# A three-block transformer on one core: instructions moved between VectorE, ScalarE and TensorE, and a new order in the second and third block

## The chip, the cores and the metric

The kernel runs on one core of a Trainium2 chip. The metric is the time of one execution on the device in microseconds (us). Three runs of the kernel before gave 1351.33, 1355.53 and 1358.17 us; the median is 1355.53. The profile shows one further execution, and all durations come from it.

Engines are called as in the profile: PE is TensorE's matrix multiply and PEld its weight load, DVE is VectorE, ACT is ScalarE, POOL is GpSimd, and SP issues the DMAs. L846 is line 846 of the kernel before. Below L742 the changed kernel has other line numbers (the old L841 is L838 there).

## The reference: what is computed

Input is `x` with 32 sequences of 128 tokens and 144 channels, and one condition vector of 144 for each sequence. Four layers follow each other, all in fp32:

- L0, an attention block with 16 heads of 9 channels. Layer norm with shift and scale from the condition; queries and keys are normalised by head; softmax; projection; then an MLP of 576 with GELU. Both results are added to `x` with a gate.
- L1, a rotation. An orthonormal basis U of 64 columns comes from a QR decomposition of a weight, and for each sequence a matrix exponential R = expm(A) of a skew 64x64 matrix that depends on the condition; then `x + (x U R - x U) U^T`.
- L2, the attention block again, without normalised queries and keys.
- L3, the attention block again, whose MLP is a mixture of 4 experts: `gate_logits = xf @ w_gate`, the best two of the four logits, a softmax over them, and the weighted sum of two experts' MLPs.

```
gate_logits = xf @ w_gate                      # [tokens, 144] x [144, 4]
topk_logits, topk_idx = top_k(gate_logits, 2)
gates = softmax(topk_logits)
```

## The kernel before, in words

**Turns and gaps.** The order of all instructions is written out by hand. A loop runs over turns (`tick` in the code, from -6 to 112). In a turn one sequence `s0` has its scores computed, the sequence of the turn before, `s1`, has them computed a second time with the maximum subtracted and exponentiated, and the one before that, `s2`, is weighed with its values, divided by the sums and projected. The first block's sequences start in turns 0 to 31, the second block's in 35 to 66, the third block's in 67 to 98. L1, the rotation, lies between the first and the second block: its QR and its exponential are prepared in pieces during the first block.

Everything else is put into named gaps of the turns, and `fill(tick, gap)` emits what was put there. The gaps of a turn follow each other as

`a, e, t, [scores half 0], stats, [weigh], b0, b, den, pre1, [scores half 1], c, y1, y2, [maxima], z, [projection]`

with "d" ahead of the maxima in the first block and after "z" from turn 35 on (the "joined" turns). `put` places a function in a gap; within a gap functions run in the order in which they were put, that is by block and by group of four sequences. `put2` splits a function at its `yield` over two gaps. Each engine executes its instructions in this program order, so a place in the list is a place in every engine's queue. [...] All PSUM results but one come from a pool of seven banks, taken in rotation.

**The pieces that the change touches.**

- `scores` (L811 to L856): TensorE computes `ps_s` (plain scores) and `ps_w` (the shifted ones, from `q2` and `kT`), L841. VectorE takes the negative maximum by head of `ps_s` into `nm` (L846), ScalarE the exponential of `ps_w` into `pr` (L853).
- `largest_T` and `largest`: TensorE transposes `nm` (L800), VectorE adds it to the queries, `q2` (L805). The next turn's `ps_w` needs `q2`.
- First block, division by the softmax sums: `sums` (L877, gap after "den") transposes the weighed values on TensorE (L881), takes the reciprocal of the sums on VectorE (L884) and spreads it over the 16 slots of a head, 128x256, on VectorE (L886, tile `rdx`). `divide_T` (after "c") transposes `rdx` on TensorE (L906), `divide` (after "y1") multiplies on VectorE into `oT` (L911), and `project_out` at the turn's end needs `oT` (L932). In the joined turns `sums_by_blocks` does it on VectorE alone.
- First block, normalised queries and keys: `qk0_T` and `qk0_project` stand in gap "c". On ScalarE they are three scalings out of `ps_qkT` (L774 to L776) and a copy and a square out of `ps_qk` (L729, L730). `qk0_guess` (gap "e") makes the first guess of a reciprocal square root from the bits of the variance with two VectorE instructions (L742, L745).
- The exponential (`prep_expm`): powers of A, then two polynomial series with 8 coefficients in 128x1024 tiles (L531, L534), then four squarings for all sequences. Further squarings stand in a conditional block that runs where a row sum of A exceeds `THETA * 16`.
- Second and third block: `qk_chunks` (turn t0 - 2, gap "c") computes queries and keys of a group of four into four banks and ScalarE copies them, `qT` (L711) and one masked half of the keys `kT` (L713). `qk_masked` writes the other masked half from the same banks on VectorE (L719, gap "z").
- Third block: `gate_logits` (L1008 to L1015, turn t0 + 7, gap "den"), `expert_ranks` one turn later, `moe1` and `moe2`, the experts' two products. `shared_by_gate` transposes the gate weights (`ps_cw`) and VectorE multiplies them into the part of `hid` that two experts share (L1077); `moe2` of an even expert reads that part in its last product (L1089) and adds to `acc` with two VectorE instructions (L1093, L1095).

Of the kernel before, what the change touches and what calls it, by code (L numbers as in the profile page):

```python
# [8 lines left out]
F32 = mybir.dt.float32  # L9
# [21 lines left out]
E = 4  # L31
G = 4
# [1 line left out]
EPS = 1e-6  # L34
SCALE = HD**-0.5

THETA = 2.0
NSQ = 18
NSQ1 = 4
KP = 80  # L40
# [26 lines left out]
def tile_kernel(ctx: ExitStack, tc: tile.TileContext, a: dict, out: bass.AP):  # L67
# [11 lines left out]
    def bank(shape, name):  # L79

        n = 1
        for s in shape[1:]:
            n *= s
        t = ps_m.tile([128, 512], F32, tag="m", name=name)
        v = t[: shape[0], :n]
        if len(shape) == 3:
            v = v.rearrange("p (a b) -> p a b", b=shape[2])
        elif len(shape) == 4:
            v = v.rearrange("p (a b c) -> p a b c", b=shape[2], c=shape[3])
        return v  # L90
# [303 lines left out]
    def prep_expm():  # L394
# [132 lines left out]
        def series(co, name):  # L527

            lo, hi = mat(f"{name}_lo"), mat(f"{name}_hi", "hi")
            for t, cs_ in ((hi, co[4:]), (lo, co[:4])):  # L530
                nc.vector.tensor_scalar(t, pw1, cs_[1], None, ALU.mult)  # L531
                yield
                for c, x in ((cs_[0], i2b), (cs_[2], pw2), (cs_[3], pw3)):
                    nc.vector.scalar_tensor_tensor(t, x, c, t, ALU.mult, ALU.add)  # L534
                    yield
            yield from products(
                pw4, hi, f"ps_{name}",
                lambda bs, ps: nc.vector.tensor_tensor(lo[:, bs, :], lo[:, bs, :], ps, ALU.add),
            )
            return lo  # L540

        even = yield from series([(-1.0) ** k / fact[2 * k] for k in range(8)], "even")
        odd = yield from series([(-1.0) ** k / fact[2 * k + 1] for k in range(8)], "odd")
        rot, rotT = mat("rot", "pow3"), mat("rotT", "pow4")

        def sum_and_difference(bs, ps):
# [192 lines left out]
    def qk0_guess(s):  # L739
        va = st[s]["va"]  # L740
        y = small.tile([128, 32], F32, tag="qky", name=f"qky_{s}", bufs=2)
        nc.vector.tensor_scalar(  # L742
            y.bitcast(I32), va.bitcast(I32), 1, None, ALU.logical_shift_right
        )
        nc.vector.tensor_scalar(y.bitcast(I32), y.bitcast(I32), -1, RSQRT, ALU.mult, ALU.add)  # L745
        st[s]["y"] = y

    def qk0_newton(s, eng=nc.gpsimd):
# [128 lines left out]
    def sums(s):  # L877

        po = st[s]["ot"][:, : 2 * T].rearrange("p (t q) -> p t q", t=2)
        for t in range(2):  # L880
            nc.tensor.transpose(po[:, t, :], st[s]["on"][:, t, :], ident)  # L881
        den = po.rearrange("p t (s c) -> p t s c", c=SLOT)[:, :, :, ONE]
        rd = small.tile([128, 2, 8], F32, tag="rd", name=f"rd_{s}")
        nc.vector.reciprocal(rd, den)  # L884
        rdx = work.tile([128, 2, 8, SLOT], F32, tag="rdx", name=f"rdx_{s}")
        nc.vector.tensor_copy(rdx, rd.unsqueeze(3).to_broadcast([128, 2, 8, SLOT]))  # L886
        st[s]["rdx"] = rdx

    def sums_by_blocks(s):

# [10 lines left out]

    def divide_T(s):
        po = st[s]["ot"][:, : 2 * T].rearrange("p (t q) -> p t q", t=2)
        rdx = st[s].pop("rdx")
        for t in range(2):
            nc.tensor.transpose(po[:, t, :], rdx[:, t, :, :].rearrange("p s c -> p (s c)"), ident)  # L906

# [100 lines left out]
    def gate_logits(g):  # L1008
        gr[g]["lg"] = lg = small.tile([128, G, E], F32, tag="lg", name=f"lg_{g[1]}", bufs=2)
        hM, hR = gr[g]["hM_m"], gr[g]["hR_m"]  # L1010
        ps = bank([128, G, E], f"ps_g_{g[1]}")
        for i in range(G):
            nc.tensor.matmul(ps[:, i, :], hM[:, i, :], L3.wgate, start=True, stop=False)
            nc.tensor.matmul(ps[:, i, :], hR[:, i, :], L3.wgateR, start=False, stop=True)
        nc.vector.tensor_copy(lg, ps)  # L1015

    def expert_ranks(g):

# [183 lines left out]
    def put2(tick, gap, to, f, *args):  # L1202

        halves = []

        def first_half():
            halves.append(f(*args))
            next(halves[0])

        def second_half():  # L1210
            for _ in halves[0]:
                pass

        put(tick, gap, first_half)
        put(tick, to, second_half)

    for layer in range(3):
        ahead = 5 if layer == 0 else 6
        for n in range(NG):
            g = (layer, n)  # L1220
            t0 = first[layer] + n * G
            for i in range(G):
                s = layer * B + n * G + i
                at_a = t0 + i - ahead
                if layer == 1 and n == 0:
                    at_a = t0 - 4 + i // 2
                if layer == 1 and i == 0:
                    put(at_a - 2, "d", rotate_T, n)
                    put(at_a - 1, "b", rotate_in, n)
                    put(at_a - 1, "d", rotate, n)  # L1230
                stats[at_a].append((s, "a"))
                stats[t0 + i + 3].insert(0, (s, "m"))
                if layer < 2:
                    put(*((at_a, "d") if at_a != t0 + i - ahead else (at_a + 1, "b")), ln_T, s, "a")
                else:
                    put(at_a, "d", ln_T, s, "a")
                if layer == 0:
                    put(t0 + i + 4, "a", ln_T, s, "m")
                else:
                    put(t0 + i + 3, "d", ln_T, s, "m")  # L1240
                if layer == 0:
                    put(t0 + i - 3, "c", qk0_project, s)
                    put(t0 + i - 3, "z", qk0_variance, s)
                    put(t0 + i - 2, "e", qk0_guess, s)
                    if s == 0:
                        for gap in "bbc":
                            put(-2, gap, qk0_newton, s, nc.vector)
                    else:
                        for gap in ("b", "c", "y2"):
                            put(t0 + i - 2, gap, qk0_newton, s)  # L1250
                    put(t0 + i - 1, "b", qk0_divide, s)
                    put(t0 + i - 1, "c", qk0_T, s)
            if layer == 0:
                for i in (0, 2):
                    put(t0 + i // 2, "b", lambda g=g, i=i: list(values(g, i, 2)))
            elif layer == 1:
                put2(t0, "stats", "b", values, g, 0, 2, True)
                put2(t0 + 1, "stats", "b", values, g, 2, 2, True)
            else:
                put2(t0, "c", "c", values, g, 0, 2, True)  # L1260
                put2(t0 + 1, "den", "pre1", values, g, 2, 2)
            if layer:
                put2(t0 - 2, "c", "c", qk_chunks, g)
                put(t0 - 2, "z", qk_masked, g)
            if layer == 0:
                put2(t0 + 10, "stats", "b", mlp1, g, 0, (0, 1, 2), True)
                put2(t0 + 11, "d", "d", mlp1, g, 3, (3, SHARED), False)
                for i in range(G):
                    put(t0 + 12 + i // 2, "bd"[i % 2], mlp2, g, i)
            elif layer == 1:  # L1270
                put2(t0 + 8, "c", "c", mlp1, g, 0, (0, 1, 2), True)
                put2(t0 + 9, "c", "c", mlp1, g, 3, (3, SHARED), True)
                for i in range(G):
                    put(t0 + (10, 10, 11, 11)[i], "bdbc"[i], mlp2, g, i)
            else:
                put(t0 + 7, "den", gate_logits, g)
                put(t0 + 8, "e", expert_ranks, g)
                put(t0 + 8, "stats", expert_weights, g)
                for i in range(G):
                    put(t0 + 8 + i // 2, "cdab"[i], moe_bias, g, i)  # L1280
                for pair in range(2):
                    at_ = t0 + 8 + 2 * pair
                    put2(at_, "stats", "b0", moe1, g, pair, 0, True)
                    put2(at_, "den", "pre1", moe1, g, pair, 1, False)
                    put2(at_ + 1, "stats", "b0", moe1, g, pair, 2, True)
                    put2(at_, "stats", "y1", shared_by_gate, g, pair)
                    put(at_, "d", moe2, g, 2 * pair, 0)
                    put(at_ + 1, "b", moe2, g, 2 * pair, 1)
                    put(at_ + 1, "c", moe2, g, 2 * pair, 2)
                    put(at_ + 1, "d", moe2, g, 2 * pair, 3)  # L1290
                    for i in range(G):
                        put(at_ + 2, "aabb"[i], moe2, g, 2 * pair + 1, i)
                put(t0 + 12, "b", moe_out, g)
# [230 lines left out]
```

## Time and profile before

| | |
|---|---|
| median of three runs | 1355.53 us |
| the profiled execution | 1347.1 us, span 1345.4 us |
| granted TensorE clock | 0.993 |
| first block, turns 0 to 33 | about 45 to 435 us |
| second block, to turn 66 | about 435 to 771 us |
| third block, turns 67 to 98 | 771 to about 1265 us, then the last experts |
| `rdx` on VectorE, L886 | 32 instructions, median 295 ns |
| second step of the guess, L745 | 32 instructions, median 217 ns |
| series, L531 and L534 | 4 of about 0.68 us and 12 of 1.2 to 1.5 us |
| gate products, L1013 and L1014 | 128 passes, 22.7 us busy |
| maxima's transpose, L800, in the joined turns | 62 instructions, 23.6 us idle before them, ended by `nm` |

A pass is one matmul instruction of the profile; an fp32 product takes two, a transpose one. Matmuls are pipelined, and a pass shows a duration longer than its distance to the next, so what a stretch costs TensorE is read from the starts. A duration on VectorE and ScalarE likewise overlaps the next instruction by up to 0.1 us. A turn takes about 10 to 13 us in the first block, about 10 us in the second, and 14 to 22 us in the third.

### The profile page before, as it was taken

The numbers are of one execution on the slowest core, as the hardware profiler recorded it, in microseconds if no ns is written. First come the engines' busy times: TensorE is split into PE (matmuls) and PEld (weight loads), VectorE is DVE, ScalarE is ACT, GpSimd is POOL, SyncE is SP. The second block draws the span as 40 slices with busy tenths as digits, with TensorE's granted clock in tenths as the row PEclk, the third lists the DMA queues.
The fourth block names the chain that finished last, engine by engine and source line by source line (L and its number), as shares of the span: only waits on it lengthen the run. The fifth ranks groups of instructions, "written<-read, shape, count | busy, mean of one in ns | idle before, by whom it ended". The sixth has DMA issues, their size and how long they took to land.

```text
span 1345.4 us, 35550 instructions
## 1 busy us (share of the span) xinstructions
PE 1275.4 (95%) x14172; PEld 935.1 (70%) x14172; DVE 821.9 (61%) x2546; ACT 821.3 (61%) x1804; POOL 642.6 (48%) x1651
## 2 busy tenths in 40 slices
PE   5999898999999989999999999999999999999997
PEld 4678587787776566766777767667676767677765
DVE  5788888867754466666766676645454545454322
ACT  2667777778856565667766666655555555555431
POOL 5677777666644333433434343526261616151632
PEclk9999999999999999999999999999999999999999
DMA  8200000000020000000100000201000000000000
GB/s 235 51 2 19 20 19 2 20 20 4 19 100 31 19 11 19 19 10 19 53 15 15 19 19 9 76 1 28 1 24 5 19 10 19 10 19 2 19 9 9
DMA packets 21671, 34.40 MB, mean 26 GB/s; under 512 B 2304, under 2 KB 12448, under 8 KB 21248
## 3 DMA queue, kind: packets, MB, share of 16 engines
q1 hardware_dynamic: 20848, 31.68, 7.9%
q8 instruction: 114, 1.87, 0.6%
q10 hardware_dynamic: 656, 0.42, 0.1%
q14 instruction: 53, 0.43, 0.1%
HBM read 29.62 MB, written 2.47 MB: 24 GB/s over the span
## 4 chain that ended last, share of the span: by engine, by line
PE 66%; DVE 7%; ACT 1%; issue 1%; POOL 0%; POOLq 0%; DVEq 0%
PE ps_h L665 19%; PE ps_f L1085 8%; PE ps_s L841 6%; PE ps_qk L665 6%; PE ps_o L868 5%; PE ps_w L841 5%; PE ps_f L958 4%; DVE nm L846 3%; PE ps_pj L932 3%; PE ps_v L665 2%; PE ps_f L1089 1%; PE ps_o L800 1%; DVE block L897 1%; DVE oT L899 1%; DVE kT L719 1%
## 5 line engine op out<-in xcount | busy, mean ns | idle before, releaser
L846 DVE TENSOR_REDUCE nm<-ps_s 128x4 f32<-128x512 f32 x384 | 246.3, 682 | 88.4 <-PE ps_w L841 77.2
L853 ACT ACTIVATE pr<-ps_w 128x512 f32<-128x512 f32 x384 | 208.6, 595 | 134.4 <-PE ps_w L841 132.9
L841 PE MATMUL ps_w<-q,kT 32*128 32x128 f32 x3072 | 234.3, 284 | 0.9 <-DVE kT L719 0.9
L841 PE MATMUL ps_s<-kT,qT 32*128 32x256 f32 x1536 | 231.5, 406 | 0.7 <-ACT kT L776 0.6
L841 PEld LDWEIGHTS ps_w<-q,kT 32*128 32x128 f32 x3072 | 197.6, 187 | 12.8 <-issue 6.2
L952 ACT ACTIVATE hid<-ps_h 128x512 f32<-128x512 f32 (+1 forms) x224 | 119.1, 591 | 105.4 <-PE ps_h L665 105.2
L918 POOL TENSOR_TENSOR x_sb<-x_sb,res_a 128x144 f32<-128x144 f32 x96 | 47.1, 490 | 255.9 <-DVE res_a L921 255.1
L841 PEld LDWEIGHTS ps_s<-kT,qT 32*128 32x128 f32 x1536 | 135.1, 184 | 28.6 <-issue 8.2
L665 PE MATMUL ps_h<-hM_m,mlps 128*128 128x512 f32 x304 | 143.8, 606 | 0.0
L1093 DVE SCALAR_TENSOR_TENSOR acc<-ps_f,cw,acc 128x144 f32<-128x144 f32 x128 | 46.6, 366 | 158.6 <-PE ps_f L1089 72.2
L868 PE MATMUL ps_o<-pr,vaug 128*32 128x128 f32 x3072 | 104.8, 277 | 0.6 <-issue 0.6
L868 PEld LDWEIGHTS ps_o<-pr,vaug 128*32 128x32 f32 x3072 | 78.6, 110 | 34.9 <-PE ps_w L841 18.5
L665 PEld LDWEIGHTS ps_h<-hM_m,mlps 128*128 128x128 f32 x304 | 53.5, 190 | 65.6 <-issue 64.2
L958 PE MATMUL ps_f<-mlps,hid 128*128 128x144 f32 x640 | 93.3, 293 | 0.0
L958 PEld LDWEIGHTS ps_f<-mlps,hid 128*128 128x128 f32 x640 | 82.5, 191 | 7.5 <-issue 4.0
L655 ACT ACTIVATE hM_m<-ps_hT_m,modM 128x128 f32<-128x128 f32 x96 | 44.5, 464 | 63.5 <-PE ps_hT_m L653 63.3
L626 POOL TENSOR_SCALAR rs_m_a<-mv_m_a 128x2 f32<-128x2 f32 x81 | 15.7, 193 | 137.2 <-DVE mv_m_a L624 109.7
L918 POOL TENSOR_TENSOR x_sb<-x_sb,res_m 128x144 f32<-128x144 f32 x64 | 32.6, 510 | 97.0 <-DVE res_m L921 96.9
L853 ACT ACT_TABLE_LOAD x57 | 73.1, 1283 | 7.0 <-PE ps_w L841 6.2
L949 ACT ACT_TABLE_LOAD x58 | 74.4, 1283 | 1.0
L1085 PEld LDWEIGHTS ps_f<-pair,hid 128*128 128x128 f32 x512 | 67.2, 191 | 8.4 <-issue 7.7
L1085 PEld LDWEIGHTS ps_f<-mlps,hid 128*128 128x128 f32 x512 | 67.2, 191 | 8.0 <-issue 6.9
(318 smaller groups left out, 2926.6 us busy)
## 6 DMA issues: line engine op xcount, KB each, us to landing
gates<-gates SPq DMA_DIRECT2D x48, 288.0 KB, 3.5
x_sb<-in_x SPq DMA_DIRECT2D x8, 288.0 KB, 9.1
out_x<-x_sb SPq DMA_DIRECT2D x8, 288.0 KB, 2.6
mlps<-in_L_mlp SPq DMA_DIRECT2D x2, 1000.0 KB, 6.2
pair<-in_L_mlp SPq DMA_DIRECT2D x1, 1800.0 KB, 10.7
mlps<-in_L_mlp SPq DMA_DIRECT2D x1, 1800.0 KB, 8.2
pow<-in_W SPq DMA_DIRECT2D x4, 320.0 KB, 6.6
mlps<-in_L_wmod SPq DMA_DIRECT2D x4, 290.0 KB, 4.8
```

What stands on the lines that cost most here:

```text
L655: nc.scalar.activation(gr[g][f"{k}_{kind}"][:, i, :], ps[:, k == "hR", :], AF.Identity, bias=m[:, sh, b : b + 1], scale=m[:, sc, b : b + 1],)
L665: nc.tensor.matmul(ps, x, y, start=k == 0, stop=k == 1)
L841: nc.tensor.matmul(o, x, y, start=True, stop=True)
L846: nc.vector.tensor_reduce(nmv[:, at0 : at0 + 2, ONE : ONE + 2], view.rearrange("p (r t k) -> p r t k", t=2, k=T), AX.X, ALU.max, negate=True,)
L853: nc.scalar.activation(pr[:, 4 * e : 4 * e + 4, :].rearrange("p s q -> p (s q)"), view, AF.Exp, scale=SCALE,)
L868: nc.tensor.matmul(po[rows4(j), t, :], v[:, 4 * j + 2 * t + r, :], prs[j // 2][:, 4 * (j % 2) + 2 * r + t, :], start=r == 0, stop=r == 1,)
L918: nc.gpsimd.tensor_tensor(x_sb[:, b, :], x_sb[:, b, :], t, ALU.add)
L949: nc.scalar.activation(t, half, AF.Gelu_apprx_tanh)
L952: nc.scalar.activation(hid[:n, i], ps[:n], AF.Gelu_apprx_tanh)
L958: nc.tensor.matmul(ps, hid[:, at0, i, :], w2[:, m, :], start=m == 0, stop=m == NFC - 1)
L1085: nc.tensor.matmul(ps[:, 0, :], hid[:, at0 + m, i, :], w2[:, at0 + m, :], start=m == 0, stop=m == 3)
L1093: nc.vector.scalar_tensor_tensor(acc, ps[:, 0, :], w, acc, ALU.mult, ALU.add)
```

## The change

In the first block the spreading of the reciprocal (`rdx`) moves from `sums` on VectorE to `divide_T` on ScalarE. The guess becomes one instruction, -0.5 times the bits plus a constant. The two series have 7 coefficients in place of 8, one accumulation less each, and their first multiplications are ScalarE's; the threshold for further squarings falls from 2.0 to 1.75 (times 16).

In the joined turns `qk_masked` moves from "z" to "y2", the third block's first `values` from "c" to "y2", and `moe2` from "d" to "y2", all ahead of the maxima's transpose.

The gate's weights are padded from 4 to 32 columns and become the stationary operand: each of the group's four sequences takes one 32-column tile of the array, its logits come out as 32 rows of one 128x128 result, ScalarE copies it to SBUF, and in gap "c" TensorE transposes it and VectorE takes the four columns of each sequence.

```diff
@@ -34,7 +34,7 @@
 EPS = 1e-6
 SCALE = HD**-0.5
 
-THETA = 2.0
+THETA = 1.75
 NSQ = 18
 NSQ1 = 4
 KP = 80
@@ -528,9 +528,9 @@
 
             lo, hi = mat(f"{name}_lo"), mat(f"{name}_hi", "hi")
             for t, cs_ in ((hi, co[4:]), (lo, co[:4])):
-                nc.vector.tensor_scalar(t, pw1, cs_[1], None, ALU.mult)
+                nc.scalar.mul(t, pw1, cs_[1])
                 yield
-                for c, x in ((cs_[0], i2b), (cs_[2], pw2), (cs_[3], pw3)):
+                for c, x in zip(cs_[:1] + cs_[2:], (i2b, pw2, pw3)):
                     nc.vector.scalar_tensor_tensor(t, x, c, t, ALU.mult, ALU.add)
                     yield
             yield from products(
@@ -539,8 +539,8 @@
             )
             return lo
 
-        even = yield from series([(-1.0) ** k / fact[2 * k] for k in range(8)], "even")
-        odd = yield from series([(-1.0) ** k / fact[2 * k + 1] for k in range(8)], "odd")
+        even = yield from series([(-1.0) ** k / fact[2 * k] for k in range(7)], "even")
+        odd = yield from series([(-1.0) ** k / fact[2 * k + 1] for k in range(7)], "odd")
         rot, rotT = mat("rot", "pow3"), mat("rotT", "pow4")
 
         def sum_and_difference(bs, ps):
@@ -739,10 +739,7 @@
     def qk0_guess(s):
         va = st[s]["va"]
         y = small.tile([128, 32], F32, tag="qky", name=f"qky_{s}", bufs=2)
-        nc.vector.tensor_scalar(
-            y.bitcast(I32), va.bitcast(I32), 1, None, ALU.logical_shift_right
-        )
-        nc.vector.tensor_scalar(y.bitcast(I32), y.bitcast(I32), -1, RSQRT, ALU.mult, ALU.add)
+        nc.vector.tensor_scalar(y.bitcast(I32), va.bitcast(I32), -0.5, RSQRT, ALU.mult, ALU.add)
         st[s]["y"] = y
 
     def qk0_newton(s, eng=nc.gpsimd):
@@ -882,9 +879,7 @@
         den = po.rearrange("p t (s c) -> p t s c", c=SLOT)[:, :, :, ONE]
         rd = small.tile([128, 2, 8], F32, tag="rd", name=f"rd_{s}")
         nc.vector.reciprocal(rd, den)
-        rdx = work.tile([128, 2, 8, SLOT], F32, tag="rdx", name=f"rdx_{s}")
-        nc.vector.tensor_copy(rdx, rd.unsqueeze(3).to_broadcast([128, 2, 8, SLOT]))
-        st[s]["rdx"] = rdx
+        st[s]["rd"] = rd
 
     def sums_by_blocks(s):
 
@@ -901,7 +896,8 @@
 
     def divide_T(s):
         po = st[s]["ot"][:, : 2 * T].rearrange("p (t q) -> p t q", t=2)
-        rdx = st[s].pop("rdx")
+        rdx = work.tile([128, 2, 8, SLOT], F32, tag="rdx", name=f"rdx_{s}")
+        nc.scalar.copy(rdx, st[s].pop("rd").unsqueeze(3).to_broadcast([128, 2, 8, SLOT]))
         for t in range(2):
             nc.tensor.transpose(po[:, t, :], rdx[:, t, :, :].rearrange("p s c -> p (s c)"), ident)
 
@@ -1008,11 +1004,16 @@
     def gate_logits(g):
         gr[g]["lg"] = lg = small.tile([128, G, E], F32, tag="lg", name=f"lg_{g[1]}", bufs=2)
         hM, hR = gr[g]["hM_m"], gr[g]["hR_m"]
-        ps = bank([128, G, E], f"ps_g_{g[1]}")
-        for i in range(G):
-            nc.tensor.matmul(ps[:, i, :], hM[:, i, :], L3.wgate, start=True, stop=False)
-            nc.tensor.matmul(ps[:, i, :], hR[:, i, :], L3.wgateR, start=False, stop=True)
-        nc.vector.tensor_copy(lg, ps)
+        ps = bank([128, T], f"ps_g_{g[1]}")
+        for w, h in ((L3.wgate, hM), (L3.wgateR, hR)):
+            for i in range(G):
+                nc.tensor.matmul(ps[rows4(i)], w, h[:, i, :], start=h is hM, stop=h is hR)
+        lgT = late.tile([128, T], F32, tag="lgT", name=f"lgT_{g[1]}")
+        nc.scalar.copy(lgT, ps)
+        yield
+        ps = bank([128, 128], f"ps_gT_{g[1]}")
+        nc.tensor.transpose(ps, lgT, ident)
+        nc.vector.tensor_copy(lg, ps.rearrange("p (i e) -> p i e", i=G)[:, :, :E])
 
     def expert_ranks(g):
 
@@ -1257,11 +1258,11 @@
                 put2(t0, "stats", "b", values, g, 0, 2, True)
                 put2(t0 + 1, "stats", "b", values, g, 2, 2, True)
             else:
-                put2(t0, "c", "c", values, g, 0, 2, True)
+                put2(t0, "y2", "y2", values, g, 0, 2, True)
                 put2(t0 + 1, "den", "pre1", values, g, 2, 2)
             if layer:
                 put2(t0 - 2, "c", "c", qk_chunks, g)
-                put(t0 - 2, "z", qk_masked, g)
+                put(t0 - 2, "y2", qk_masked, g)
             if layer == 0:
                 put2(t0 + 10, "stats", "b", mlp1, g, 0, (0, 1, 2), True)
                 put2(t0 + 11, "d", "d", mlp1, g, 3, (3, SHARED), False)
@@ -1273,7 +1274,7 @@
                 for i in range(G):
                     put(t0 + (10, 10, 11, 11)[i], "bdbc"[i], mlp2, g, i)
             else:
-                put(t0 + 7, "den", gate_logits, g)
+                put2(t0 + 7, "den", "c", gate_logits, g)
                 put(t0 + 8, "e", expert_ranks, g)
                 put(t0 + 8, "stats", expert_weights, g)
                 for i in range(G):
@@ -1284,10 +1285,10 @@
                     put2(at_, "den", "pre1", moe1, g, pair, 1, False)
                     put2(at_ + 1, "stats", "b0", moe1, g, pair, 2, True)
                     put2(at_, "stats", "y1", shared_by_gate, g, pair)
-                    put(at_, "d", moe2, g, 2 * pair, 0)
+                    put(at_, "y2", moe2, g, 2 * pair, 0)
                     put(at_ + 1, "b", moe2, g, 2 * pair, 1)
                     put(at_ + 1, "c", moe2, g, 2 * pair, 2)
-                    put(at_ + 1, "d", moe2, g, 2 * pair, 3)
+                    put(at_ + 1, "y2", moe2, g, 2 * pair, 3)
                     for i in range(G):
                         put(at_ + 2, "aabb"[i], moe2, g, 2 * pair + 1, i)
                 put(t0 + 12, "b", moe_out, g)
@@ -1476,7 +1477,8 @@
         mlp(f"L3_{n}", w1, b1, w2)
     arrays["L3_b2"] = inputs["L3_cond_b2"].ravel()
     w = inputs["L3_cond_w_gate"]
-    main_and_rest("L3_wgate", w, np.zeros(E, w.dtype), 1)
+    w = np.pad(w, ((0, 0), (0, 32 - E)))
+    main_and_rest("L3_wgate", w, np.zeros(32, w.dtype), 1)
 
 
 
```

## The prediction

> **What bounds the kernel now.** I read four views: the page's engine shares and chain, the windows by stage, the timeline of single turns, and the waits.
>
> ```profile
> PE 1275.4 (95%) x14172; PEld 935.1 (70%) x14172; DVE 821.9 (61%) x2546; ACT 821.3 (61%) x1804; POOL 642.6 (48%) x1651
> ...
> PE 66%; DVE 7%; ACT 1%; issue 1%; POOL 0%; POOLq 0%; DVEq 0%
> ```
>
> TensorE is the bound: busy 95%, and 66% of the chain, against 7% for VectorE. So an edit is worth what it does to the time between TensorE's instructions, and work taken off VectorE pays only where TensorE waits for VectorE.
>
> ```profile
> 45.00:435.00 390.00, 367.67 (x4967) 283.71 (x4965) 297.32 (x1009) 279.84 (x738) 253.16 (x722) 0.99 0.08 26
> 435.00:771.00 336.00, 321.40 (x3746) 229.27 (x3743) 213.52 (x590) 220.94 (x434) 129.52 (x320) 0.99 0.07 20
> 771.00:1265.00 494.00, 481.19 (x4705) 346.18 (x4704) 264.68 (x769) 283.77 (x536) 204.02 (x461) 1.00 0.06 18
> ```
>
> The columns are the stretch, its length, then busy time of PE, PEld, DVE, ACT, POOL. The stretches are the first, second and third attention block. VectorE is at 76% in the first, 64% and 54% in the others; TensorE is at 94 to 97% in all.
>
> **Part 1: the spread reciprocal moves to ScalarE (first block).** The line to judge is where the copy stands in its new queue. In the old kernel VectorE writes `rdx` (L886) before the second half of the scores. In the new one ScalarE writes it in `divide_T`, after everything the "c" gap gave ScalarE. One turn, TensorE, VectorE, ScalarE:
>
> ```profile
> 289.05 0.39 PE L841 MATMUL ps_w<-q,kT 32*128 32x128 f32 x4
> ...
> 290.83 0.38 PE L906 MATMUL ps_o<-cst,rdx 128*128 128x128 f32 x2
> 291.05 1.39 PE L958 MATMUL ps_f<-mlps,hid 128*128 128x144 f32 x10
> ...
> 288.73 0.29 DVE L886 COPY rdx<-rd 128x256 f32<-128x256 f32 x1
> ...
> 289.55 1.09 ACT L853 ACTIVATE pr<-ps_w 128x512 f32<-128x512 f32 x2 [0.31 <-PE ps_w L841]
> ...
> 291.59 0.43 ACT L729 COPY qkraw<-ps_qk 128x288 f32<-128x288 f32 x1
> 291.87 0.46 ACT L730 ACTIVATE qksq<-ps_qk 128x288 f32<-128x288 f32 x1
> ```
>
> The reader should see that TensorE transposes `rdx` at 290.83, 1.5 us after the last score, while ScalarE, released by the same score, still has two exponentials, three scalings, a copy and a square to do, until 292.33. The new copy comes behind them. Its nearest row is ScalarE's `on` copy of the same 128x256 at 0.375 us; with the overlap of 0.09 us between neighbours on ScalarE and 0.05 us to wake TensorE it ends 0.33 us after the square, at 292.66. TensorE works its queue in order (no matmul overtakes another in the timeline), so the transposes and all behind them (the second MLP product, the transpose of the maxima, the projection, the next scores) wait 292.66 - 290.83 = 1.83 us. Nothing carries over: ScalarE is idle from 292.33 to 293.68 and starts the next turn in step.
>
> I read the 32 turns alike: end of the last ScalarE instruction of that gap, plus 0.33, minus the start of L906. 24 turns give 1.2 to 1.8, mean 1.71, together 41.0. Six have a table load in front of the exponentials (L730 starts 154.85, so ready 155.64 against 152.61, 3.03) or a late start: mean 2.97, together 17.8. One gives 0.5, the last none. **Sum 59.3 us.**
>
> Part of it covers waits that TensorE has anyway in this block:
>
> ```profile
> PE ps_qr L327 <- DVE at L353: 7.8, 6, 2.4
> PE ps_pj L932 <- DVE oT L911: 7.4, 8, 1.1
> PE ps_yr L371 <- DVE at L353: 1.5, 1, 1.5
> ```
>
> With two smaller ones (1.1 and 1.0) they make 18.8 us. In the table-load turn these waits are 0.99 and 1.92: delayed by 3.03, the projection starts 2.4 later instead, because `oT` still needs the transposes and 0.42 us on VectorE; VectorE's later chain moves by about 1.0, so the second wait all but goes. There 2.1 of 2.9 us are covered. I take three quarters of 18.8, 14 us. Ends: everything paid, 59; or double the covered time (the weight loads list waits of the same kind, PEld on `oT` 8.6 and on `at` 3.9), 31. **Part 1: +45, from +31 to +59.**
>
> [...]
>
> **Part 2: VectorE work dropped.** One instruction less in `qk0_guess` (32 x 0.15 to 0.22), four 128x1024 multiplications of 0.68 us to ScalarE and two accumulations of 1.27 to 1.5 us gone from the series: with `rdx` some 21 us of VectorE. What TensorE waited for VectorE is already counted above, so I take 0. Ends: -5 if more of it was on the path, +4 for ScalarE's four multiplications at about 1.1 us (twice the 0.59 of a 128x512 copy, less an overlap) if each delays a turn. The series ends two gaps earlier, so the same squarings fill other gaps: 0. The squaring threshold 28 instead of 32 changes no step: I worked out the row sums of the skew matrices from the inputs, and the largest is 26.8.
>
> **Part 3: gate logits in column tiles.** Old: 16 passes with 4 columns each, each after a full weight load: first start 967.13, next matmul 968.91, 1.78 us, eight times. New: 16 passes in four column tiles; `ps_o` (L868) does 32 passes of the same shape in 1.01 us, so 0.5 us, plus one transpose at 0.11. Saved 1.17 x 8 = **-9.4**. Without overlap of the tiles 16 x 0.115 = 1.84 us, +1.4 in all. ScalarE's copy in between is hidden by the second scores and one MoE product (2.3 us).
>
> **Part 4: order in the joined turns.** The views are the turns around 936 and 958:
>
> ```profile
> 935.78 0.33 PE L800 MATMUL ps_o<-cst,nm 128*128 128x128 f32 x1 [1.22 <-DVE nm L846]
> ...
> 960.22 0.37 PE L841 MATMUL ps_w<-q,kT 32*128 32x128 f32 x1
> ...
> 958.45 0.41 DVE L805 TENSOR_TENSOR q<-qT,ps_o 128x256 f32<-128x256 f32 x1
> 958.87 1.41 DVE L719 TENSOR_SCALAR kT<-ps_qk,cst 128x512 f32<-128x512 f32 x2
> ```
>
> (a) `moe2` (1.25 us) moves ahead of the transpose L800, into its wait for the maxima. Six turns like the first line give 1.25 each, six give about 0.6 (waits of 0.52), two single ones 0.7 and 0.9: **-12.7**. What follows has 3 us of other work before `q` is needed. Ends -13 and -4 (a new wait for `q` behind the two accumulations).
> (b) `qk_masked` moves ahead of `q` on VectorE. It must wait for ScalarE's `kT`, which reads the same banks (10.0 us of waiting in ten turns now), then takes 1.41 us; `q`, which the next scores need, comes behind. Around 958 the queue becomes: cw product to 958.5, `moe2` sums until 959.65 (TensorE ends `moe2` near 959.0), `kT` to 961.0, `q` to 961.4. The first `ps_w` went at 960.22, so TensorE waits 1.2 us more, in five turns. Where no MoE runs yet the same sum gives 0.4 (around 598: `kT` ends 598.47, `q` 598.8, while the scores were held until 598.5 by the bank that `kT` frees), in ten turns. **+10**, from 0 to +15.
> (c) `values` of the third block behind the cw transposes: `moe2` then reaches the shared product a little before VectorE has `hid`, and `q` stands behind four copies: about 0.25 in six turns, **+1.5**, from -3 to +5.
>
> **Sum.** 45 + 0 - 9.4 - 12.7 + 10 + 1.5 = +34 on the profiled execution of 1347.1 us (span 1345.4), 1381. That execution is 0.6% under the median of the runs, 1355.53; on that, 1390.
>
> **Rivals.**
> R1, not slower: VectorE holds the first block, and the wait at L906 only takes the place of waits for VectorE. For: VectorE is busy 297 of 390 us there. Against: TensorE's waits for it are 18.8 us, a third of the 59. It needs 48 of the 59 covered, under 0.35 us left per turn. With part 1 at 0 and 10 gained on VectorE: 1355.5 - 10 - 9.4 - 12.7 + 11.5 = 1335.
> R2, the reorder costs nothing: if (b) and (c) find `q` in time, 1390 - 11.5 = 1379. For: TensorE's scores were held by `kT` already. Against: ScalarE's `kT` comes late in every such turn.
> R3, nothing covered: 59 in part 1 and (a) at -4: 1390 + 14 + 9 = 1413. For: most turns (the one shown) have no later wait above 0.4 us.
> R4, the threshold lets the conditional squarings run: four now take 9.3 us of TensorE, so fourteen 33 us and more, 1423 and up. Against: 26.8 is below 28.
>
> **How the numbers follow.** Forecast as worked out 0.60, R2 0.17, R3 0.15, R1 0.06, R4 0.02. The forecast is 1390. The range 1366 to 1412 leaves out R1, R4, and the tails of R2 and R3: part 1 at 31 with the reorder free gives 1390 - 14 - 11 = 1365, and R3 is at its upper edge. About 0.5% (7 us) is what this kernel's measurement can tell from no change: faster 0.04, same 0.04 (R1 and its border), slower 0.92.
>
> **What would show it.** Part 1: the first block, 390 us from 45 to 435, becomes about 435; its `rdx` transposes show idle time ended by ScalarE's `rdx`, some 1.8 us each, above any other TensorE wait. Part 3: the gate takes 0.6 us where it took 1.8. Part 4: L800's wait for `nm` in the third block falls from 12.8 us to under 3, and `ps_w` waits for `q` behind `kT`. Wrong would be: the `rdx` wait short because TensorE arrives late at it, held by something I took as covered; or the joined turns longer by more than 1 us each.

## The result and the profile after

The changed kernel takes 1407.80 us (median of four runs, 1401.98 to 1410.80), where the kernel before takes 1355.49 us: ratio 1.038, 95% interval 1.034 to 1.042, so 52 us slower. The profiled execution of the changed kernel took 1401.98 us, its span is 1400.3 us.

The engine shares and the chain of the changed kernel, from the page:

```profile
PE 1281.8 (92%) x14180; PEld 928.1 (66%) x14180; DVE 799.9 (57%) x2476; ACT 836.3 (60%) x1848; POOL 644.6 (46%) x1651
...
PE 32%; DVE 1%; issue 0%; POOLq 0%; POOL 0%
```

VectorE is busy 22 us less, as the edits intend, and TensorE's share falls from 95% to 92%: it works about as long as before (1282 us against 1275) and waits longer. The chain's shares add up to 33% here and to 75% before, so it reaches back over different parts of the two executions, and its 32% can't be set against the 66% before. The eight passes more than before are the eight transposes of the gate's logits; the conditional squarings did not run.

The windows by stage (stretch, length, busy time of PE, PEld, DVE, ACT and POOL, then the granted clock), with bounds at the same places of the work as those shown of the kernel before:

```profile
49.00:499.00 450.00, 379.85 (x4966) 288.46 (x4964) 278.25 (x935) 294.07 (x775) 254.82 (x718) 0.95 0.08 23
499.00:837.00 338.00, 318.80 (x3746) 226.60 (x3747) 212.90 (x592) 218.82 (x432) 129.37 (x320) 1.00 0.07 20
837.00:1322.00 485.00, 476.48 (x4716) 336.33 (x4715) 261.81 (x767) 286.99 (x545) 205.03 (x464) 1.00 0.06 18
```

The first block grew from 390 to 450 us, the second from 336 to 338, and the third fell from 494 to 485. In the first block TensorE's clock was granted at 0.95, before at 0.99. TensorE's waits in the first block of the changed kernel:

```profile
PE ps_o L902 <- ACT rdx L900: 62.3, 32, 3.8
PE ps_pj L928 <- PEq L586: 3.7, 1, 3.7
PE ps_pj L928 <- DVE oT L907: 2.3, 6, 0.4
PE ps_yr L371 <- DVE at L353: 0.7, 1, 0.7
```

All 32 transposes of `rdx` now wait for ScalarE (the single wait at L586 is at the conditional block of the squarings, not at the copy). The old waits for VectorE, `ps_qr` 7.8 and `ps_pj` 7.4, are down to nothing and 2.3. The turn that the prediction showed, in the timeline of the changed kernel:

```profile
325.32 0.49 ACT L773 ACTIVATE kT<-ps_qkT,cst 128x256 f32<-128x256 f32 x1
...
325.68 0.43 ACT L729 COPY qkraw<-ps_qk 128x288 f32<-128x288 f32 x1
...
325.95 0.46 ACT L730 ACTIVATE qksq<-ps_qk 128x288 f32<-128x288 f32 x1
326.26 0.45 ACT L900 COPY rdx<-rd 128x256 f32<-128x256 f32 x1
326.76 0.44 PE L902 MATMUL ps_o<-cst,rdx 128*128 128x128 f32 x2 [1.67 <-ACT rdx L900]
```

The copy starts behind the square and ends at 326.71; the transposes follow 0.05 us later.

### The profile page after: what moved, and what is told of

It reads as the page before. It is cut to its first block, busy times and chain, and to the rows that moved or that the text cites. A ratio compares the mean times of both kernels' runs of the same rounds, so it can differ in the third digit from the quotient of the medians.

```text
span 1400.3 us, 35516 instructions
## 1 busy us (share of the span) xinstructions
PE 1281.8 (92%) x14180; PEld 928.1 (66%) x14180; DVE 799.9 (57%) x2476; ACT 836.3 (60%) x1848; POOL 644.6 (46%) x1651
## 5 line engine op out<-in xcount | busy, mean ns | idle before, releaser
L838 PE MATMUL ps_s<-kT,qT 32*128 32x256 f32 x1536 | 237.3, 414 | 0.0
L838 PEld LDWEIGHTS ps_s<-kT,qT 32*128 32x128 f32 x1536 | 138.7, 189 | 30.1 <-issue 9.4
L665 PEld LDWEIGHTS ps_h<-hM_m,mlps 128*128 128x128 f32 x304 | 53.4, 190 | 65.6 <-issue 64.7
L954 PEld LDWEIGHTS ps_f<-mlps,hid 128*128 128x128 f32 x640 | 83.6, 193 | 7.6 <-issue 4.0
L635 POOL TENSOR_SCALAR xr<-x_sb,rs_m_a 128x64 f32<-128x64 f32 x162 | 79.9, 493 | 0.0
L1086 PEld LDWEIGHTS ps_f<-pair,hid 128*128 128x128 f32 x512 | 66.9, 190 | 8.4 <-issue 7.7
```

The source lines that it names most:

```text
L635: nc.gpsimd.tensor_scalar(xr.rearrange("p (k c) -> p k c", k=4)[:, :, :CR], x_sb[:, b, CM:].unsqueeze(1).to_broadcast([128, 4, CR]), minus ...
L665: nc.tensor.matmul(ps, x, y, start=k == 0, stop=k == 1)
L838: nc.tensor.matmul(o, x, y, start=True, stop=True)
L954: nc.tensor.matmul(ps, hid[:, at0, i, :], w2[:, m, :], start=m == 0, stop=m == NFC - 1)
L1086: nc.tensor.matmul(ps[:, 0, :], hid[:, at0 + m, i, :], w2[:, at0 + m, :], start=m == 0, stop=m == 3)
```

## The experiments

Some measures recur. The *gap* is the time from the start of TensorE's last instruction ahead of the `rdx` transposes to their start, summed over the 32 turns (in e8, which has added work there, the last instruction ahead of that work). A *turn* runs from one transpose of the maxima to the next. "First block" in this section is the time from the first of these transposes to the 33rd, which belongs to the second block's first sequence; "the third block with the tail" runs from the second block's last transpose of the maxima to the end; lost clock is one minus the granted clock, times the time. Ratios are against the kernel before in the same set of runs (medians 1356.3 for the first four, 1356.5 for the next four, 1353.1 for the last two).

### The copy alone, and the copy undone

One kernel has only the copy, the other everything but the copy. The extracts of the code in this section show the lines that decide.

```diff
 # e1: the kernel before, and
-        nc.vector.tensor_copy(rdx, rd.unsqueeze(3).to_broadcast([128, 2, 8, SLOT]))  # in sums
+        nc.scalar.copy(rdx, rd.unsqueeze(3).to_broadcast([128, 2, 8, SLOT]))  # in divide_T
 # e2: the changed kernel, and
-        nc.scalar.copy(rdx, rd.unsqueeze(3).to_broadcast([128, 2, 8, SLOT]))  # in divide_T
+        nc.vector.tensor_copy(rdx, rd.unsqueeze(3).to_broadcast([128, 2, 8, SLOT]))  # in sums
```

> The kernel before with one edit: the spread of the reciprocal goes from VectorE in `sums` to ScalarE in `divide_T`; nothing else changes. Queue theory: the wait of 1.83 us per turn at the transposes of `rdx` is the whole loss of the first block, so this kernel alone is 52 to 66 us slower than before, about 1415 us, and the idle time before those transposes is about 62 us. Rival (a good part of the first block's 64 us comes from the other small edits there or from the lower granted clock of that stretch): 30 to 45 us slower, with the same 62 us of idle time.

> The changed kernel with `rdx` back on VectorE in `sums`; all other edits stay. Queue theory: the first block is back at its old length or a few us below it, and the 9 us that the joined turns and the tail gained remain: 1340 to 1349 us, ratio 0.989 to 0.995. Rival (something else lengthens the first block): at or above 1355 us.

The copy alone: 1418.7 us, ratio 1.049 (1.043 to 1.054), 62 us slower than the kernel before. The copy undone: 1347.1 us, ratio 0.994 (0.991 to 0.997), 61 us faster than the changed kernel. So the copy is more than the whole loss, and the rest of the change is a small gain.

### Same engine, another place in its queue

The same copy stays on ScalarE, ahead of the exponentials, or behind them but ahead of gap "c".

```diff
 # e3: the copy in sums, where VectorE's stood
+        nc.scalar.copy(rdx, rd.unsqueeze(3).to_broadcast([128, 2, 8, SLOT]))  # in sums
-        nc.scalar.copy(rdx, rd.unsqueeze(3).to_broadcast([128, 2, 8, SLOT]))  # in divide_T
 # e10: the copy after the second half of the scores (spread holds it; first block only)
         scores(s0, s1, 1)
+        spread(s2)                                 # nc.scalar.copy(rdx, rd.unsqueeze(3).to_broadcast([128, 2, 8, SLOT]))
         fill(tick, "c")
         divide_T(s2)
```

> The changed kernel with `rdx` on ScalarE, but written in `sums`, that is ahead of the exponentials of the second half in ScalarE's queue. Queue theory: ScalarE has the reciprocal at about the time it is free, the copy of 0.45 us ends before the exponentials can start, and the transposes wait for nothing: within 8 us of the kernel with the copy on VectorE, 1340 to 1355 us. Rival (ScalarE is too loaded in this block for the copy, wherever it stands): above 1380 us.

> The changed kernel with ScalarE's rdx copy a few places further up its queue: behind the exponentials of the second scores, but ahead of the three scalings, the copy and the square of gap c. Queue theory: the copy ends about 1.5 us earlier than in the changed kernel, so 25 ordinary turns wait about 0.2 us and the six with a table load about 1.5, together 14 us where the changed kernel's gap grew by 67, and much of it is covered: 1347 to 1355, close to the 1347 and 1350 of the two versions without the wait. Rival (it is the work that ScalarE does later in the turn that costs: the queries and keys now come out later behind the copy): 32 x 0.4 us more on ScalarE's side, 1360 or more. If any idle time in the block brings the half-clock windows, the lost clock stays near 20 us; by the queue theory it falls to about 5 to 9.

| | gap, us | first block, us | lost clock, us | ratio to before |
|---|---|---|---|---|
| before (VectorE) | 8.0 | 401.7 | 5.1 | 1 |
| e2, VectorE | 8.1 | 404.6 | 8.5 | 0.994 |
| e3, ScalarE ahead of the exponentials | 8.3 | 401.2 | 5.1 | 0.996 |
| e10, ScalarE ahead of gap "c" | 24.6 | 409.3 | 6.8 | 1.003 |
| changed kernel, ScalarE after gap "c" | 74.9 | 461.7 | 21.6 | 1.038 |

The engine costs nothing that these runs can tell (the intervals of e3 and e2 overlap); the place costs 61 us. e10 lies between: 16.5 us more gap than e2 go with 4.8 us more of the first block. The fastest executions of the two differ by as much (1347.4 and 1342.5, and e10's trace is of its fastest), but by the ratios e10 takes 0.9% longer, some 12 us. Its median, 1359.9, is 5 us above what was expected of it and at the lower edge of its rival, that the queries and keys come out later behind the copy. So the time alone doesn't exclude that rival for e10, and where the other 7 us are stays open; no trace was kept of its slower executions. Waits of e10 in the first block:

```profile
PE ps_o L906 <- ACT rdx L899: 12.8, 11, 2.3
PE ps_pj L932 <- DVE oT L911: 4.9, 8, 1.3
PE ps_pj L932 <- PEq L586: 4.1, 1, 4.1
PE ps_qr L327 <- DVE at L353: 3.1, 4, 1.5
```

The waits for the copy are down to 11, six of them in turns with a table load (1.28 us on ScalarE in the trace of the kernel before), and the old waits for VectorE come back in part. This is how cover looks in a profile: as one wait shrinks, another returns.

### Work put into the wait

The block's clock fell to 0.95, which the prediction has no term for. This kernel fills the wait with transposes that nobody reads.

```diff
     def divide_T(s):
         nc.scalar.copy(rdx, rd.unsqueeze(3).to_broadcast([128, 2, 8, SLOT]))
+        for _ in range(14):
+            nc.tensor.transpose(st[s]["ot"][:, 2 * T : 3 * T], ident, ident)
         for t in range(2):
             nc.tensor.transpose(po[:, t, :], rdx[:, t, :, :].rearrange("p s c -> p (s c)"), ident)
```

> The changed kernel, with 14 transposes of the identity (about 0.11 us each, 1.5 us together) ahead of the rdx transposes in each turn of the first block. They write PSUM columns that nobody reads, so this is added work, and the output is unchanged. TensorE still has to wait for ScalarE's copy to the same moment, but it is busy in most of the wait. Clock theory: of the changed kernel's +52 us against before, some 13 us are half-clock windows that the idle waits of the first block bring on. Then the first block's lost clock falls from about 20 us to about 5, the wait left at the rdx transposes is about 0.3 us a turn, and the median is near 1395, against 1408 without the filling, though TensorE does 48 us more work. Rival (the windows come from something else, or by chance): lost clock stays at 17 to 21 us and the time is 1408 or more; a third outcome, 14 x 0.11 x 32 = 49 us more, would mean that the transposes of rdx had not been waiting at all.

It took 1402.8 us, ratio 1.035 (1.030 to 1.041). The gap is the same, 75.0 us, and most of it is filled: 10.5 us of the 62.3 us of waiting are left. Waits of e8 in the first block, and its window (bounds again at the same places):

```profile
PE ps_o L904 <- ACT rdx L900: 10.5, 9, 2.3
```

```profile
54.00:499.00 445.00, 420.24 (x5414) 331.72 (x5413) 280.11 (x937) 294.06 (x777) 251.25 (x718) 0.98 0.07 23
```

TensorE is busy 40 us more and the block is 5 us shorter (450 to 445). From the first maxima on, the lost clock of the block falls from 21.6 to 8.5 us and its time from 461.7 to 456.2. One trace could show that by chance: kernels without the waits lost between 3.4 and 13.1 us there. The whole executions are better evidence, as each has its mean clock (span times one minus the clock, mean over the runs):

| | runs | lost clock, us | median, us |
|---|---|---|---|
| before, in three sets | 23, 29, 17 | 14.7, 10.4, 10.4 | 1353 to 1357 |
| e2, e3, e10 (short or no wait) | 12, 10, 12 | 16.9, 16.2, 15.1 | 1347 to 1360 |
| e4, e5, e6, e7, e9 (below; no wait for the copy) | 6, 12, 12, 12, 6 | 15.4, 14.2, 14.7, 16.3, 18.0 | 1333 to 1358 |
| changed kernel | 4 | 27.4 | 1407.8 |
| e1, the copy alone | 4 | 30.5 | 1418.7 |
| e8, the waits filled | 6 | 19.1 | 1402.8 |

Some 9 to 15 us of lost clock come with the idle waits. The firmest comparison is e1's 30.5 against the 15.4 to 16.9 of e2, e3 and e4, which were run beside it on one chip. With the waits filled the mean is 8 lower than the changed kernel's and near e9's 18.0, which has no such wait. That the filling takes it away is likely and not settled: single executions lost 18.3 to 38.0 in the changed kernel and 11.2 to 26.7 in e8, and the two come from different sets of runs, while the kernel before itself lost 14.7 in one set and 10.4 in two others. The time gains 5, less than the 13 expected. That running slower costs nothing where TensorE then waits for ScalarE anyway would explain it, but no run shows this alone. That the time falls at all rests on medians 5.0 us apart with overlapping intervals and on the 5.4 us of the two traces.

### The parts of the second and third block

Three kernels have one part alone, and one is e2 with the keys put back as well.

```diff
 # e5: the kernel before with the gate's column tiles alone
 # e6: the kernel before, and
-                    put(at_, "d", moe2, g, 2 * pair, 0)
+                    put(at_, "y2", moe2, g, 2 * pair, 0)
-                    put(at_ + 1, "d", moe2, g, 2 * pair, 3)
+                    put(at_ + 1, "y2", moe2, g, 2 * pair, 3)
 # e7: the kernel before with the guess, the series and THETA alone
 # e4: e2, and
-                put(t0 - 2, "y2", qk_masked, g)
+                put(t0 - 2, "z", qk_masked, g)
```

> The kernel before, with only the gate's weights in column tiles. By part 3 of the prediction 8 x 1.17 = 9.4 us less: 1347 where before is 1356. In each group of the third block the turn that holds the gate is shorter by about 1.2 us, the other three as before. Rival (the column tiles do not run side by side, or ScalarE's copy and the transpose come out on the path): 0 to +2 us, so 1356 to 1358.

> The kernel before, with only the two moe2 pieces moved from d (after the maxima) to y2 (ahead of their transpose). By part 4 (a) of the prediction 12.7 us less, 1343 where before is 1356: two of the four turns of each group in the third block are shorter, by 1.25 and 0.6. Rival (the wait for the maxima only moves, to q behind the two accumulations on VectorE): 4 us less, 1352. A second rival from the trace of the changed kernel, where only one turn of four is much shorter (1.26) and the one with the shared keys 0.5: here, with the keys late, both of at_ + 1 are 1.2 shorter, the two of at_ none, so 14 turns x 1.2 = 17 us less at most.

> The kernel before, with only the one-instruction guess, the two series with 7 coefficients and their first multiplications on ScalarE, and the lower threshold. By part 2 of the prediction 0 us (from -5 to +4): 1356. Rival (VectorE holds the first block, so each microsecond taken off it is worth one): 12 us less, 1344. A rival in which the lower threshold lets the conditional squarings run: 24 us more at least.

> As the kernel with `rdx` back on VectorE, and the masked keys (`qk_masked`) also back in gap z, behind the new queries. Forecast of the prediction, part 4 (b): the joined turns lose the waits of `ps_w` for `q`, 5 turns of 1.2 us and 10 of 0.4, so 10 us less than that kernel, about 1334 us. Rival (the scores were held by the bank that the masked keys free, in either order): no difference within 3 us.

| | median, us | ratio to before, 95% interval |
|---|---|---|
| e5, gate alone | 1344.97 | 0.992 (0.988 to 0.996) |
| e6, `moe2` alone | 1346.73 | 0.994 (0.991 to 0.997) |
| e7, small edits alone | 1358.47 | 1.003 (0.999 to 1.006) |
| e4, e2 with the keys late | 1338.86 | 0.990 (0.985 to 0.995) |

The gate. TensorE's timeline of the changed kernel, in the group whose old gate took 1.78 us:

```profile
1031.10 0.43 PE L1010 MATMUL ps_g<-hM_m,L_wgate 128*32 128x128 f32 x8
1031.34 0.40 PE L1010 MATMUL ps_g<-hR_m,L_wgateR 128*32 128x128 f32 x8
1031.67 0.48 PE L838 MATMUL ps_s<-kT,qT 32*128 32x256 f32 x2
```

From 1031.10 to 1031.67 is 0.57 us. In e5 the turn with the gate falls from 14.44 to 13.29, 1.15 less (in the first one 1.60), and the third block and the tail together are 9.5 us shorter.

`moe2` ahead of the maxima. Waits of the third block, e6 (the kernel before has 12.8 us here for `nm`):

```profile
PE ps_o L800 <- DVE nm L846: 1.4, 2, 0.8
PE ps_w L841 <- ACT hR_a L655: 0.9, 4, 0.2
PE ps_f L1089 <- DVE hid L1077: 0.4, 1, 0.4
```

The waits for the maxima are down to 1.4 us, but a group of four turns went only from 13.93 + 21.79 + 14.45 + 18.41 = 68.58 to 12.85 + 21.93 + 14.23 + 18.49 = 67.50, and the third block with the tail from 583.5 to 576.6, 6.9 us. The first of these turns gave 1.1, close to the 1.25 counted. The third, in which the keys of the next group are masked, gave 0.2 where 0.6 was counted, and the other two grew by 0.14 and 0.08. In the kernel before, the bulk of the third turn's shifted scores follows the first projection after 0.96 us (959.38 to 960.34), in e6 after 1.54 (958.78 to 960.32), so TensorE gives back there what it saved. What it waits for there is in the timeline of e6, with one line of the kernel before at the end:

```profile
958.23 0.27 PE L800 MATMUL ps_o<-cst,nm 128*128 128x128 f32 x1
...
959.06 0.41 DVE L805 TENSOR_TENSOR q<-qT,ps_o 128x256 f32<-128x256 f32 x1
...
959.62 0.37 PE L841 MATMUL ps_w<-q,kT 32*128 32x128 f32 x1
...
959.80 0.46 ACT L655 ACTIVATE hR_a<-ps_hT_a,modR 128x128 f32<-128x128 f32 x1
...
960.32 0.38 PE L841 MATMUL ps_w<-q,kT 32*128 32x128 f32 x2 [0.21 <-ACT hR_a L655]
```

```profile
960.40 0.46 ACT L655 ACTIVATE hR_a<-ps_hT_a,modR 128x128 f32<-128x128 f32 x1
```

`q` is ready at 959.47. The profile puts the wait down to `hR_a`, the last output of the layer norm on ScalarE, which ends at 960.26; the second line of the wait list is this wait, in four turns, one in each of four groups. In the kernel before, the scores go on at 960.34 and `hR_a` ends at 960.86, so there they didn't wait for it. Why they do in e6 the profile doesn't name, and no run shows it.

The keys ahead of the queries. Timeline of the changed kernel, VectorE and TensorE around one such turn:

```profile
1022.08 0.30 DVE L1096 TENSOR_TENSOR acc<-acc,ps_f 128x144 f32<-128x144 f32 x1
1022.30 1.40 DVE L719 TENSOR_SCALAR kT<-ps_qk,cst 128x512 f32<-128x512 f32 x2
...
1023.62 0.41 DVE L802 TENSOR_TENSOR q<-qT,ps_o 128x256 f32<-128x256 f32 x1
...
1024.17 0.38 PE L838 MATMUL ps_w<-q,kT 32*128 32x128 f32 x2 [0.87 <-DVE q L802]
```

`q` stands behind 1.40 us of keys, and the scores wait 0.87 us for it. Put back, these turns are 0.74 us shorter in the third block (13.97 to 13.23) and 0.34 in the second (10.48 to 10.14). By the medians of e2 and e4 the edit costs 8.3 us. By their traces it is 8.9 from the second block on; e2's trace has one half-clock stretch more there (1.7 us of lost clock).

### A version that beats both

It is e4 with two more moves undone. The gate, the small edits and the last `moe2` piece of each pair stay.

```diff
-                put2(t0, "y2", "y2", values, g, 0, 2, True)
+                put2(t0, "c", "c", values, g, 0, 2, True)
-                    put(at_, "y2", moe2, g, 2 * pair, 0)
+                    put(at_, "d", moe2, g, 2 * pair, 0)
                     put(at_ + 1, "y2", moe2, g, 2 * pair, 3)
```

> The changed kernel with four things undone: rdx on VectorE, qk_masked back in z, the third block's first values back in c, and the first moe2 piece of each pair back in d; only the last moe2 piece (at_ + 1) stays ahead of the maxima. Kept are the gate in column tiles and the small edits. From the turns: a group of four in the third block took 68.6 us in the kernel before, the gate takes 1.15 off it and the one moe2 piece 1.1 to 1.3, so 66.1 to 66.3, against 66.6 with the four undone only in part (rdx and the keys). Six groups give 2 to 3 us less than that version's 1338.9: 1336, some 20 under the kernel before and 72 under the changed one. Rival (values and the first moe2 piece cost nothing where they are, or the piece in d opens the wait for the maxima again): 1339 or more.

It took 1332.7 us, ratio 0.985 (0.981 to 0.989): 20 us faster than the kernel before. A group of four turns takes 65.6 us against 66.6 in e4, the third block with the tail 563.1 against 568.7, and the wait list of its third block has one line left:

```profile
PE ps_o L797 <- DVE nm L843: 1.8, 3, 0.8
```

## Why the prediction was right, and which terms were off

The forecast was 1390, the measurement 1407.8: the direction, the cause and its place were right, and the sum of +34 was 18 us short of +52. The two larger misses, the clock and the wait in part 1 and the gain in part 4 (a), went the same way, and the result lies 4 us under the upper end of the range. Term by term:

- **Part 1, the wait (59.3).** The mechanism is shown by e1, e2, e3 and e10. Its size by the traces is the growth of the gap, 74.9 - 8.0 = 66.9. Ordinary turns have 2.08 - 0.24 = 1.84, the 1.83 of the turn that was worked out, where the mean of the 24 was taken as 1.71. The copy takes 0.45 us on ScalarE (median of the 32), not the 0.375 of its nearest row, and overlaps the square by 0.16, not 0.09, so the transposes start 0.35 us after the square where 0.33 was counted; neighbours on ScalarE overlap by up to 0.22 us in the two traces, not by 0.1. The last turn, counted at nothing, has 3.19 - 0.52 = 2.7.
- **Part 1, the cover (14).** Of the changed kernel's gap with work put into it, against e2 at the same lost clock of 8.5 us, the first block grew by 456.2 - 404.6 = 51.7. So 66.9 - 51.7 = 15.2 us were covered, if the filling itself cost nothing. The three quarters of 18.8 were a fair guess, though the traces of e10 and e2 show that the share isn't the same at every size of wait: 11.7 of 16.5 us.
- **Part 1, the clock, which had no term.** "Nothing carries over" was said of the queues, and holds there. But TensorE's clock falls with the waits, and the changed kernel's block loses 13.1 us more than e2's. I put the 5.4 us that e8 takes away down to that. 66.9 - 15.2 + 5.4 = 57.1, which is the difference of the first block between the changed kernel and e2; that it comes out is no check, since the last two terms were both taken from these traces. A second pair of traces, e1 and the kernel before, differs by 59.5 there. Part 1 was +45 and is +57 to +59 by the traces, +61 by the medians. The traces can't tell such differences better: the start alone, up to the first transpose of the maxima, took from 46.8 to 57.1 us in traces of kernels with the same code there.
- **Part 2 (0).** e7: -0.1 to +0.6%. None, though VectorE is busy 10 us less. That VectorE at 76% isn't the bound of the first block is thereby shown.
- **Part 3 (-9.4).** -9.5 by the traces of e5 and -11.5 by medians.
- **Part 4 (a) (-12.7).** -6.9 by the traces of e6 and -8.0 by its ratio. The step that failed is "What follows has 3 us of other work before `q` is needed". In the first kind of turn that holds (935.78 to 940.17, less the 1.25 moved away). In the turns with the keys 1.4 us are left (958.23 to 959.62 in e6), and then the scores stand until 960.32, not for `q` but, by the profile, for ScalarE's `hR_a`. The lower end, -4, was named for a wait for `q`.
- **Part 4 (b) (+10).** +8.3 by medians. The wait is 0.87 us and the turn loses 0.74, where 1.2 was counted: four passes of the plain scores now go ahead of the shifted ones, where it was two.
- **Part 4 (c) (+1.5).** Undone together with the first `moe2` piece it gave 5.7 us between the traces of e4 and e9 (third block with the tail), and 6 by their medians. How much is `values` was not run alone.

Of the rivals, R1 falls with e1 and R4 with the count of TensorE's instructions. R2 falls with e4. R3's 1413 is nearer to the result than the forecast, but not for its reasons: 15 us were covered, and what was missing was the last turn's wait and the clock.

All the parts together, traces against traces: first block 57.1 for the copy and 2.9 between before and e2 (e2's block has 3.4 us more lost clock, two half-clock stretches); the joined turns and the tail -9.2; the start +4.1. The sum is 54.9, the difference of the two spans.

## What to carry to other kernels

Work that is moved to a less busy engine is worth what its place in that engine's queue makes of it: look in the timeline at what the new engine does at the moment the result is needed, not at its busy share. The same copy on the same engine cost 61 us at the end of a gap and nothing measurable ahead of the exponentials. And parts of a change are to be run one by one: this one, 52 us slower as a whole, held 20 us of gain.

## What the runs showed of the hardware

In the traces of the kernel before and the changed kernel, TensorE's granted clock is 1 or 0.5, and the half-clock stretches last 3.41 us or a multiple of it (13.65 at most), but for the one at the end of each trace (3.68 and 5.87). In turns that are otherwise the same, one such stretch costs 1.6 us (turn 43: 8.88 us without in the changed kernel, 10.50 with in the kernel before). Executions with waits of mostly 1.7 us by the wait list, one each turn, lost 27 and 30 us on average, where kernels without them lost 10 to 18. The longest single wait doesn't order them. In the wait lists of the first block it is 3.8 us in the changed kernel (for the copy) and 2.9 in e1 (up to 437 us), and 3.8 and 3.7 in e2 and e3, both at L586. On average e1 lost the most, 30.5 us (its traced execution 22.5, the changed kernel's 29.2), e2 and e3 16.9 and 16.2. So in these runs the loss went with waits in every turn, not with one long wait. What decides the single stretch stays open: kernels without these waits have some in the same block too (the kernel before has three, 5.1 us of lost clock), at places that differ from run to run.
